# A message-passing network on one core: the messages' preparations move into the second convolution, and the edges' ends come in long rows that TensorE transposes

## The chip, the cores and the metric

The kernel runs on one core of a Trainium2 chip. The metric is the device time of one execution in microseconds (us). The engines are called PE (TensorE, the matrix engine; PEld is its weight load), DVE (VectorE), ACT (ScalarE), POOL (GpSimd) and SP (SyncE, which only issues transfers here). A PEq, ACTq or SPq in a row of the profile is that engine's issuing of a transfer.

## The reference

A graph of N = 6250 nodes with D = 64 features and E = 206250 directed edges (100,000 random pairs in both directions and a loop at each node), sorted by destination. Four layers, each behind a layer norm and a ReLU, each added to x:

```python
h = jnp.maximum(_layernorm(x, axis=-1), 0.0)
x = x + _L0_gnn_ref(h, edge_index, W3, b3, W4, b4)      # relu(S h W3' + b3) W4' through S again, S = D^-1/2 (A+I) D^-1/2
h = jnp.maximum(_layernorm(x, axis=-1), 0.0)
x = x + _L1_gnn_ref(h, edge_index)                      # sums over neighbours, scaled by deg^-1/2 on both sides
h = jnp.maximum(_layernorm(x, axis=-1), 0.0)
x = x + _L2_gnn_ref(h, edge_attr_64, src, dst, ...)     # messages, below
h = jnp.maximum(_layernorm(x, axis=-1), 0.0)
x = x + _L3_gnn_ref(edge_index, h)                      # three more neighbour sums (LightGCN), averaged
```

The third layer has work for each edge:

```python
Vp = leaky_relu(leaky_relu(V) @ pAw + pAb) @ pBw + pBb
x = relu(relu(E @ w1 + b1) @ w2 + b2)                   # E: 64 attributes of each edge
msg = sigmoid(x @ Bw + Bb) * Vp[src] + (x @ Cw + Cb)
M = clip(msg, 1e-5, None) ** 2
mean = segment_sum(M, dst) / max(cnt, 1)
return mean ** 0.5
```

## The kernel before

**Tiles.** Nodes are padded to 49 blocks (`NB`) of 128, in 7 chunks (`NC`) of 7 blocks (`CB`). A node matrix is a tile of 128 x 49 x 64. The graph is a dense matrix `A` of edge counts in fp8, in HBM, 7 column chunks of 128 x 49 x 896. A *piece* is one 7-block part of a chunk (784 KB). For the messages the edges are cut into 202 groups (`G`) of 1024: 128 partitions with 8 edges (`J`) each, consecutive in memory.

**Stages**, all in the function `fast`, with the times of the profiled execution:

1. *0 to 585 us.* `A` is built: pairs of source and destination go to HBM, runs of them are gathered, one-hot matrices are multiplied (L853), strips of `A` are evicted and stored (L984). On each strip the first convolution's neighbour sum runs (`convolve`, with `spread`, L748), then the hidden layer (`hidden`, L944 to L968); its last chunk ends the stage.
2. *585 to 806, gather 1* (the second convolution's neighbour sum). `gather` (L998) loops over 7 chunks of 7 pieces: SP loads a piece (L1007, eight buffers), PE multiplies it with node features split in three bf16 parts (L1013; L1010 is a multiplication with zeros that opens a bank), DVE sums the parts (L1021) and the function handed in, `convolved` (L1035), adds the bias and the residual and makes the next layer norm.
3. *806 to 1038, gather 2*, the same with `turned` (L1053): residual, layer norm (`normed`, L691 to L703), transposes (`p_node`, L1062), the two multiplications of Vp (`p_a` L1067, `p_v` L1073), the bias (`v`, L1076 and L1078) and the store of Vp to HBM (L1079).
4. *1038 to 1084, the preparations of the messages* (L1092 to L1157), below.
5. *1084 to 3670, the messages.* A schedule written by hand for PE, ACT and DVE: `slot(i)` for 202 groups in a pipeline seven deep. `loaded` brings edge attributes `e` (L1270, SP), `fetched` issues eight indirect transfers of Vp rows by `src_g` (L1276, POOL), `turned_edges` transposes `e` (`p_e`, L1284), two layers follow (L1288, L1292), gates and shifts (`p_bc`, L1298 and L1302), the message (DVE, L1311 to L1313), its sum by destination (`p_s`, L1330) with a one-hot matrix made of `lane` and `count`. Between these steps each slot takes a share of a list of other work: *crossings*, which compare pieces of `A` with their mirror images (`piece` L1177, `there` L1182, `p_sum` L1185, `junk` L1191), and partial sums of the first LightGCN layer. A chunk of nodes whose edges are all summed is `finished`.
6. *3670 to 4140.* The rest of LightGCN layer 1, and two more gathers.

`general`, which follows, runs only if `fast` has found that the graph isn't what it assumes; it isn't run here.

**The preparations.** ACT issues the loads of weights into diagonals (`w1_d`, `w2_d`) and `BC`, and eight small loads of biases (L1109, L1110); DVE splits the biases into three bf16 parts (L1113 to L1117); SP moves these to the rows of `BC_b` (L1120). SP loads the two index arrays, source and destination of each edge, group by group along a partition: partition p gets, of each of 202 groups, the 8 indices p·8 to p·8+7, so 128 x 202 runs of 32 bytes for each array:

```python
nc.sync.dma_start(src_g, src.rearrange("(g p j) -> p g j", p=P, j=J))
nc.sync.dma_start(dst_g, dst.rearrange("(g p j) -> p g j", p=P, j=J))
```

POOL writes `origin`, the first node of each group's window (194 memsets, L1133), and `count` (L1154). DVE makes from `dst_g` the check that all destinations lie in their windows (`rel`, `off`, `missed`, L1136 to L1142) and `lane` (L1145, L1147), all of 128 x 1616 elements.

**What sets the order.** Outside of the hand-written part the framework orders each engine's instructions by their dependencies and its own estimates; so preparations that wait for nothing are issued before gather 2's last chunk is through. An engine runs its instructions, the issuing of transfers among them, in that order and stops at the first that must wait. Tiles lie in pools. A pool opened where a closed one lay waits for all of that one's readers, writers and transfers. `cpool` (what the messages read) and `tpool` (what only the preparations need) lie where gather 2's buffers were.

Of the kernel before, what the change touches and what calls it, by code (L numbers as in the profile page):

```python
# [11 lines left out]
I32 = mybir.dt.int32  # L12
# [587 lines left out]
def window(g):  # L600

    per = N / E
    lo = max(int(g * P * J * per) - DRIFT, 0) // QN
    hi = min(int((g + 1) * P * J * per) + DRIFT, NP - 1) // QN
    assert hi - lo < P // QN
    return lo
# [10 lines left out]
def fast(ctx, tc, bad, x, src, dst, edge_attr, W3, b3, W4, b4, w1, b1, w2, b2, Bw, Bb, Cw, Cb,  # L617
# [48 lines left out]
    node = ctx.enter_context(tc.tile_pool(name="node", bufs=1))  # L666
    stat = ctx.enter_context(tc.tile_pool(name="stat", bufs=2))
# [84 lines left out]
    nc.scalar.dma_start(X, x.rearrange("(b p) f -> p b f", p=P))  # L752
    early = ExitStack()
    early_pool = early.enter_context(tc.tile_pool(name="early_pool", bufs=1))
    with ExitStack() as ph:

        ipool = ph.enter_context(tc.tile_pool(name="ipool", bufs=1))
        with ExitStack() as first:
            dpool = first.enter_context(tc.tile_pool(name="dpool", bufs=1))
# [37 lines left out]
        npool = looked.enter_context(tc.tile_pool(name="npool", bufs=1))  # L797
# [11 lines left out]
        rpool = ph.enter_context(tc.tile_pool(name="rpool", bufs=3))  # L809
        opool = ph.enter_context(tc.tile_pool(name="opool", bufs=2))  # L810
        spool = ph.enter_context(tc.tile_pool(name="spool", bufs=2))
        wpool = ph.enter_context(tc.tile_pool(name="wpool", bufs=1))
# [13 lines left out]
        with ExitStack() as ps:  # L826
            psum = ps.enter_context(tc.tile_pool(name="ps0", bufs=1, space=PSUM))
# [198 lines left out]

    with ExitStack() as ph:
        wpool = ph.enter_context(tc.tile_pool(name="wpool", bufs=2))  # L1030
        U3 = of_nodes(node)
        with tc.tile_pool(name="apool", bufs=8) as apool, \
                tc.tile_pool(name="ps1", bufs=1, space=PSUM) as psum:

            def convolved(c, z):  # L1035
                add_whole(z, V3, c)
                nc.vector.tensor_mul(z, z, over_features(norm0[:, blocks(c)]))
                nc.vector.tensor_add(z, z, over_blocks(b4_r, CB))
                nc.vector.tensor_add(X[:, blocks(c), :], X[:, blocks(c), :], z)
                h = wpool.tile([P, CB, D], F32, name="h")  # L1040
                normed_and_split(h, U3, c, norm3)

            gather(apool, wpool, psum, V3, convolved)
# [6 lines left out]
        with tc.tile_pool(name="apool", bufs=8) as apool, \  # L1050
                tc.tile_pool(name="ps2", bufs=1, space=PSUM) as psum:
# [34 lines left out]
    late = ctx.enter_context(tc.tile_pool(name="late", bufs=1))  # L1086
    H = late.tile([P, NB, D], F32, name="H")
    U3 = of_nodes(node)
    part = ctx.enter_context(tc.tile_pool(name="part", bufs=1))
    Y = part.tile([P, CS, CW], F32, name="Y")  # L1090
    piece_pool = ctx.enter_context(tc.tile_pool(name="piece_pool", bufs=3))
    with ExitStack() as ph:  # L1092
        cpool = ph.enter_context(tc.tile_pool(name="cpool", bufs=1))
        before = ExitStack()
        tpool = before.enter_context(tc.tile_pool(name="tpool", bufs=1))
        w1_d = diagonal(w1, "w1_d")
        w2_d = diagonal(w2, "w2_d")
        b1_c = column(b1, 2, "b1_c")
        b2_c = column(b2, 2, "b2_c")

        BC = cpool.tile([P, 4 * D], F32, name="BC")
        nc.vector.memset(BC, 0.0)
        for k in range(2):
            nc.scalar.dma_start(BC[k * D:(k + 1) * D, 2 * k * D:(2 * k + 1) * D], Bw)
            nc.scalar.dma_start(BC[k * D:(k + 1) * D, (2 * k + 1) * D:(2 * k + 2) * D], Cw)

        bias = tpool.tile([1, 4, 2, D], F32, name="bias")
        for k in range(4):
            nc.scalar.dma_start(bias[:, k, 0, :], Bb.unsqueeze(0))  # L1109
            nc.scalar.dma_start(bias[:, k, 1, :], Cb.unsqueeze(0))  # L1110
        rest = tpool.tile([1, 4, 2, D], F32, name="rest")
        bias3 = [tpool.tile([1, 4, 2, D], BF16, name=f"bias{k}") for k in range(3)]
        nc.vector.tensor_copy(bias3[0], bias)  # L1113
        nc.vector.tensor_sub(rest, bias, bias3[0])
        nc.vector.tensor_copy(bias3[1], rest)
        nc.vector.tensor_sub(rest, rest, bias3[1])
        nc.vector.tensor_copy(bias3[2], rest)  # L1117
        BC_b = cpool.tile([3, 8 * D], BF16, name="BC_b")
        for k in range(3):
            nc.sync.dma_start(BC_b[k:k + 1, :], bias3[k].rearrange("o a b f -> o (a b f)"))  # L1120
        ones = cpool.tile([3, P], BF16, name="ones")
        nc.vector.memset(ones, 1.0)

        src_g = cpool.tile([P, G, J], I32, name="src_g")
        nc.sync.dma_start(src_g, src.rearrange("(g p j) -> p g j", p=P, j=J))
        dst_g = tpool.tile([P, G, J], I32, name="dst_g")
        nc.sync.dma_start(dst_g, dst.rearrange("(g p j) -> p g j", p=P, j=J))

        origin = tpool.tile([P, G], F32, name="origin")
        g0 = 0  # L1130
        for g in range(1, G + 1):
            if g == G or window(g) != window(g0):
                nc.gpsimd.memset(origin[:, g0:g], float(window(g0) * QN))  # L1133
                g0 = g
        rel = tpool.tile([P, G, J], F32, name="rel")
        nc.vector.tensor_tensor(rel, dst_g, origin.unsqueeze(2).to_broadcast([P, G, J]),  # L1136
                                op=OP.subtract)
        off = tpool.tile([P, G, J], F32, name="off")
        nc.vector.tensor_scalar(off, rel, float(P), None, op0=OP.is_ge)
        nc.vector.tensor_scalar(rel, rel, 0.0, None, op0=OP.is_lt)  # L1140
        nc.vector.tensor_add(off, off, rel)
        nc.vector.tensor_reduce(missed[:, 1:2], off.rearrange("p g j -> p (g j)"), axis=AX.X,  # L1142
                                op=OP.add)

        nc.vector.tensor_scalar(dst_g, dst_g, P - 1, None, op0=OP.bitwise_and)  # L1145
        lane = cpool.tile([P, G, J], BF16, name="lane")
        nc.vector.tensor_copy(lane, dst_g)  # L1147
        own = cpool.tile([P, P // QN, 2], F32, name="own")
        nc.vector.memset(own[:, :, 0], 0.0)
        for q in range(P // QN):  # L1150
            nc.vector.memset(own[q * QN:(q + 1) * QN, :q + 1, 0], 1.0)
        nc.vector.tensor_scalar(own[:, :, 1], own[:, :, 0], -1.0, 1.0, op0=OP.mult, op1=OP.add)
        count = cpool.tile([P, P, J], BF16, name="count")
        nc.gpsimd.iota(count, pattern=[[1, P], [0, J]], base=0, channel_multiplier=0,  # L1154
                       allow_small_or_imprecise_dtypes=True)

        before.close()  # L1157
        mpool = ph.enter_context(tc.tile_pool(name="mpool", bufs=3))
        ps_a = ph.enter_context(tc.tile_pool(name="ps_a", bufs=1, space=PSUM))
# [255 lines left out]


# [87 lines left out]
```

## Time and profile before

| | us |
|---|---|
| median of 8 runs | 4152.68 |
| lowest, highest | 4138.55, 4200.15 |
| the profiled execution | 4141.91 |
| its span in the profile | 4140.0 |

Busy in the profiled span: PE 3170.8 us (77%), PEld 2173.4 (52%), DVE 1978.2 (48%), ACT 1258.3 (30%), POOL 1654.7 (40%). The granted TensorE clock is 0.85 of full speed on average.

The views used below are these. The *page's slices* cut the span in 40 equal parts, one digit each: the busy share in tenths (9 is 90% or more); PEclk is the TensorE clock that the throttle granted, DMA the mean busy share of the core's 16 DMA engines. *Busy time by stretch* gives for a stretch of the span each engine's busy us and its number of instructions, the granted clock, the DMA share and GB/s. The *timeline* has one row for a run of like instructions: start, length, engine, line, operation, output and inputs, count, and in brackets how long the engine stood idle before and what ended that. A busy time is not a bound: what a stage costs is read from the engine or transfer that the others wait for in that stage.

### The profile page before, as it was taken

How to read it: one execution, taken by the hardware profiler on the slowest of the kernel's cores; microseconds unless marked ns; L12 is line 12 of the kernel's file. 1: busy time of each engine (PE TensorE's matmuls, PEld its weight loads, DVE VectorE, ACT ScalarE, POOL GpSimd, SP SyncE). 2: the span in 40 equal slices, each digit the busy share in tenths (PEclk: the TensorE clock that was granted, in tenths of full speed). 3: DMA queues.
4: the chain of work that ended last, by engine and by line, in shares of the span. 5: the costliest groups of instructions: out<-in, count | busy, mean ns of one | idle time of the engine just before them, and what ended most of it. 6: DMA issues, size and time to landing. Idle time of an engine off the chain costs nothing.

```text
span 4140.0 us, 59188 instructions
## 1 busy us (share of the span) xinstructions
PE 3170.8 (77%) x24193; PEld 2173.4 (52%) x24193; DVE 1978.2 (48%) x3904; ACT 1258.3 (30%) x2031; POOL 1654.7 (40%) x1870
## 2 busy tenths in 40 slices
PE   1699999999366656777677677677767776789999
PEld 1466669999233333444333344344434343459999
DVE  5899953322344444545444444545445454461111
ACT  1577740000133333333333333333333333320000
POOL 4100000000466665665565666666566656510000
PEclk9799999999677777777877778878877788799999
DMA  3233346554722222222222222222222222236664
GB/s 102 71 83 88 100 147 196 183 183 132 93 58 58 60 58 55 74 66 72 56 58 78 57 66 68 65 73 61 75 58 64 60 74 63 53 107 194 196 202 151
DMA packets 280495, 388.75 MB, mean 94 GB/s; under 512 B 189225, under 2 KB 191331, under 8 KB 279955
## 3 DMA queue, kind: packets, MB, share of 16 engines
q1 hardware_dynamic: 222260, 323.17, 25.9%
q0 software_dynamic: 54112, 58.92, 7.2%
q8 instruction: 192, 3.15, 0.3%
q10 hardware_dynamic: 3840, 2.77, 0.3%
q14 instruction: 91, 0.75, 0.1%
HBM read 340.47 MB, written 44.24 MB: 93 GB/s over the span
## 4 chain that ended last, share of the span: by engine, by line
PE 51%; DVE 17%; another core or an unknown queue 12%; issue 9%; ACT 7%; DMA 2%; POOL 1%; DVEq 0%; ACTq 0%; POOLq 0%; SPq 0%
PE p_acc L1013 18%; PE p_sum L748 9%; PE p_bc L1302 6%; PE p L1288 5%; PE p_a L853 3%; ACT h L1292 2%; DVE junk L1191 2%; DVE m L1312 2%; DVE m L1311 2%; PE p_s L1330 2%; PE p_bc L1298 2%; PE p_e L1284 2%; DVE m L1313 1%; DVE m L1374 1%
## 5 line engine op out<-in xcount | busy, mean ns | idle before, releaser
L1276 POOL DMA_INDIRECT v<-Vp_dram,src_g x1616 | 1592.1, 985 | 997.9 <-DVE m L1311 490.0
L1013 PE MATMUL p_acc<-U,piece 128*128 128x192 bf16 x9604 | 816.8, 247 | 3.1 <-DMA piece<-A 3.1
L1013 PEld LDWEIGHTS <-piece 128*128 128x128 fp8e4 x9604 | 799.2, 98 | 14.8 <-DMA piece<-A 3.7
L1302 PE MATMUL p_bc<-BC,h 128*128 128x256 f32 x1616 | 580.2, 490 | 9.9 <-issue 9.6
L1311 DVE TENSOR_TENSOR m<-gate,v 128x512 f32<-128x512 f32 x202 | 139.9, 693 | 675.5 <-ACT gate L1307 472.0
L1302 PEld LDWEIGHTS p_bc<-BC,h 128*128 128x128 f32 x1616 | 339.5, 233 | 170.0 <-issue 132.7
L1185 PE MATMUL p_sum<-ident_b,piece 128*128 128x128 bf16 x1372 | 159.2, 240 | 337.8 <-DVE junk L1191 301.0
L1191 DVE SCALAR_TENSOR_TENSOR junk<-p_sum,there 128x512 bf16<-128x512 f32 (+1 forms) x392 | 241.9, 617 | 349.4 <-remote 249.8
L748 PEld LDWEIGHTS <-U 128*64 128x64 bf16 x4116 | 236.9, 114 | 316.1 <-issue 179.9
L1185 PEld LDWEIGHTS <-piece 128*128 128x128 fp8e4 x1372 | 120.0, 108 | 490.9 <-issue 474.6
L1133 POOL MEMSET origin<- 128x1 f32 (+1 forms) x194 | 6.5, 97 | 907.4 <-PE p_acc L1013 907.4
L1021 DVE TENSOR_REDUCE zg<-p_acc 128x128 f32<-128x384 f32 x112 | 56.9, 508 | 599.6 <-PE p_acc L1013 599.0
L857 ACT ACTIVATE strip<-p_a 128x784 fp8e4<-128x784 f32 x392 | 302.0, 820 | 120.8 <-PE p_a L853 103.7
L748 PE MATMUL p_sum<-piece,U 128*64 128x448 fp8e4 x2058 | 268.5, 387 | 89.7 <-issue 56.9
L1288 PE MATMUL p<-h,w_d 128*128 128x512 f32 x404 | 269.4, 750 | 63.0 <-ACT h L1292 53.6
L1292 ACT ACTIVATE h<-p,b_c 128x512 f32<-128x512 f32 x404 | 261.5, 683 | 173.1 <-remote 58.4
L1298 PE MATMUL p_bc<-BC_b,ones 3*128 3x512 bf16 x404 | 183.7, 455 | 135.9 <-DVE m L1312 129.0
L1330 PE MATMUL p_s<-m,to 128*128 128x192 bf16 x1616 | 207.9, 278 | 101.4 <-DVE r_s L1338 55.4
L1375 ACT ACTIVATE m<-m 128x512 bf16<-128x512 f32 x202 | 127.3, 630 | 520.5 <-DVE m L1374 390.6
L1318 ACT ACTIVATE m<-m 128x512 bf16<-128x512 f32 x202 | 127.2, 630 | 434.2 <-DVE m L1313 341.3
L1298 PEld LDWEIGHTS <-ones 3*128 3x128 bf16 x404 | 37.6, 93 | 417.6 <-issue 216.5
L1288 PE MATMUL p<-eT,w_d 128*128 128x512 f32 x404 | 246.6, 695 | 11.9 <-ACT h L1292 7.1
(189 smaller groups left out, 3650.8 us busy)
## 6 DMA issues: line engine op xcount, KB each, us to landing
piece<-A SPq DMA_DIRECT2D x249, 784.0 KB
e<-in_edge_attr SPq DMA_DIRECT2D x202, 256.0 KB
A<-strip SPq DMA_DIRECT2D x14, 2744.0 KB
v<-Vp_dram,src_g POOLq DMA_INDIRECT x1616
there<-A SPq DMA_DIRECT2D x28, 784.0 KB
pairs<-pair SPq DMA_DIRECT2D x1, 1616.0 KB
Vp_dram<-v SPq DMA_DIRECT2D x7, 224.0 KB
out<-X SPq DMA_DIRECT2D x6, 224.0 KB
```

What stands on the lines that cost most here:

```text
L748: nc.tensor.matmul(p[half * D:(half + 1) * D, :w], U3[:, b, k, :], at_block, start=(i < 2), stop=(i >= 3 * n - 2))
L857: nc.scalar.activation(strips[s][:, :, col:col + 2 * SG].rearrange("p b (j l) -> p b j l", l=2), p[:, :, :2 * NB].rearrange("p j (b l) -> ...
L1013: nc.tensor.matmul(p[d // 2][:, d % 2 * 3 * D:(d % 2 + 1) * 3 * D], t[:, b, d * P:(d + 1) * P], U3[:, k * CB + b, :, :].rearrange("p t f - ...
L1185: nc.tensor.matmul(p[:, a - a0, :], held["here"][:, a, b * P:(b + 1) * P], ident_b, start=True, stop=True)
L1191: nc.vector.scalar_tensor_tensor(junk[:, :(a1 - a0) * P], p[:, :a1 - a0, :].rearrange("p a q -> p (a q)"), 15.5, there, op0=OP.min, op1=OP ...
L1276: nc.gpsimd.indirect_dma_start(out=v[:, j, :], out_offset=None, in_=Vp_dram[:, :], in_offset=bass.IndirectOffsetOnAxis(ap=src_g[:, g, j:j ...
L1288: nc.tensor.matmul(of[g][p], w, of[g].pop(x), start=True, stop=True)
L1292: nc.scalar.activation(of[g][t], of[g].pop(p), **how)
L1298: nc.tensor.matmul(p_bc[:, 4 * b:4 * b + 4].rearrange("p j o f -> p (j o f)"), ones, BC_b, start=True, stop=False)
L1302: nc.tensor.matmul(p_bc[:, 2 * q:2 * q + 2].rearrange("p j o f -> p (j o f)"), h2[:, q * P:(q + 1) * P], BC, start=False, stop=(k == 1))
L1311: nc.vector.tensor_mul(m, of[g].pop("gate"), of[g].pop("v"))
L1330: nc.tensor.matmul(p, to[:, :, j], m3[:, j].rearrange("p t f -> p (t f)"), start=(j == 0), stop=(j == J - 1))
```

## The change

The preparations become a function, `prepared(psum)`, which `convolved` calls when it gets chunk 1 of gather 1. Its tiles lie at the other end of SBUF (`side="right"`), and `cpool` stays open until the messages are over. The transfers into `BC_b` are issued by ACT instead of SP. The index arrays come as rows: a group is one row of 1024 indices, 4 KB; 101 groups, half an array, are one transfer, issued by ACT. DVE casts such a half to float32 with the 8 indices of a partition drawn apart, PE transposes it in eight pieces of 101 x 128, four to a PSUM bank (32 transposes in all), and ACT writes each four back as integers into `src_g` or `dst_g`. All that follows from these two tiles is as it was. Beside that, all pools of `fast` get `reuse_waits="tile"`: a tile waits for those earlier tiles whose memory it takes, no longer for the whole closed pool; and `spool` (the strips of `A`) goes to the right side.

```diff
-    node = ctx.enter_context(tc.tile_pool(name="node", bufs=1))
-    stat = ctx.enter_context(tc.tile_pool(name="stat", bufs=2))
+    node = ctx.enter_context(tc.tile_pool(name="node", bufs=1, reuse_waits="tile"))
+    stat = ctx.enter_context(tc.tile_pool(name="stat", bufs=2, reuse_waits="tile"))
...
+    apart = ctx.enter_context(ExitStack())
     early = ExitStack()
...
-        spool = ph.enter_context(tc.tile_pool(name="spool", bufs=2))
+        spool = ph.enter_context(tc.tile_pool(name="spool", bufs=2, side="right", reuse_waits="tile"))
...
+    def prepared(psum):
+
+        cpool = apart.enter_context(tc.tile_pool(name="cpool", bufs=1, side="right", reuse_waits="tile"))
+        before = ExitStack()
+        tpool = before.enter_context(tc.tile_pool(name="tpool", bufs=1, side="right", reuse_waits="tile"))
+        w1_d = diagonal(w1, "w1_d")
...
+        BC_b = cpool.tile([3, 8 * D], BF16, name="BC_b")
+        for k in range(3):
+            nc.scalar.dma_start(BC_b[k:k + 1, :], bias3[k].rearrange("o a b f -> o (a b f)"))
...
+        src_g = cpool.tile([P, G, J], I32, name="src_g")
+        dst_g = tpool.tile([P, G, J], I32, name="dst_g")
+        GH = G // 2
+        for ends, t in ((src, src_g), (dst, dst_g)):
+            for h in range(2):
+                rows_i = tpool.tile([GH, P, J], I32, name="rows_i", bufs=2)
+                nc.scalar.dma_start(rows_i, ends[h * GH * P * J:(h + 1) * GH * P * J].rearrange(
+                    "(g p j) -> g p j", p=P, j=J))
+                rows_f = tpool.tile([GH, J, P], F32, name="rows_f", bufs=2)
+                nc.vector.tensor_copy(rows_f, rows_i.rearrange("g p j -> g j p"))
+                for j0 in range(0, J, 4):
+                    p = psum.tile([P, 4, GH], F32, name="p_turn", bufs=2)
+                    for j in range(4):
+                        nc.tensor.transpose(p[:, j, :], rows_f[:, j0 + j, :], ident[:GH, :GH])
+                    nc.scalar.activation(
+                        t[:, h * GH:(h + 1) * GH, j0:j0 + 4],
+                        p.rearrange("p j g -> p g j"), AF.Copy)
...
+        before.close()
+        return cpool, w1_d, w2_d, b1_c, b2_c, BC, BC_b, ones, src_g, lane, own, count
+
+    made = []
...
             def convolved(c, z):
+                if c == 1:
+                    made.append(prepared(psum))
                 add_whole(z, V3, c)
...
-        BC_b = cpool.tile([3, 8 * D], BF16, name="BC_b")
-        for k in range(3):
-            nc.sync.dma_start(BC_b[k:k + 1, :], bias3[k].rearrange("o a b f -> o (a b f)"))
...
-        src_g = cpool.tile([P, G, J], I32, name="src_g")
-        nc.sync.dma_start(src_g, src.rearrange("(g p j) -> p g j", p=P, j=J))
-        dst_g = tpool.tile([P, G, J], I32, name="dst_g")
-        nc.sync.dma_start(dst_g, dst.rearrange("(g p j) -> p g j", p=P, j=J))
...
+        cpool, w1_d, w2_d, b1_c, b2_c, BC, BC_b, ones, src_g, lane, own, count = made.pop()
+        mpool = ph.enter_context(tc.tile_pool(name="mpool", bufs=3, reuse_waits="tile"))
...
+    apart.close()
```

## The prediction

> **What bounds the kernel now.** I read the page's slices first, to see which engine fills which stage, then busy time by stage, then the timeline at the two seams that the change touches.
>
> ```profile
> PE   1699999999366656777677677677767776789999
> DVE  5899953322344444545444444545445454461111
> PEclk9799999999677777777877778878877788799999
> DMA  3233346554722222222222222222222222236664
> ```
>
> A slice is 103.5 us. Counted from 1, TensorE (PE) is full in slices 3 to 10 (first convolution, then the two gathers) and in the last four (layers); slices 12 to 36, the messages, have no full engine. Slice 11 is the hole: PE 3, and DMA 7, the highest of its row. The stages in numbers (after span and length: PE, PE weight loads, DVE, ACT, POOL busy; granted clock; DMA share; GB/s):
>
> ```profile
> 580.00:815.00 235.00, 225.96 (x2560) 217.04 (x2554) 78.75 (x145) 14.17 (x28) 0.00 (x0) 0.96 0.56 184
> 1040.00:1120.00 80.00, 22.44 (x79) 12.48 (x79) 19.91 (x40) 6.46 (x11) 36.28 (x180) 0.60 0.90 110
> 1120.00:1320.00 200.00, 125.48 (x501) 70.89 (x502) 86.48 (x189) 66.75 (x112) 124.83 (x129) 0.72 0.23 58
> 1320.00:3600.00 2280.00, 1616.63 (x7468) 900.02 (x7468) 1097.99 (x2422) 773.50 (x1293) 1412.67 (x1431) 0.79 0.25 64
> ```
>
> Gather 1 is PE's own: 226 of 235 us. What the change puts on PE there lengthens it; what it puts on DVE (79 of 235 busy) or POOL (0) does not. The stretch before the messages is bound by DMA. Its timeline (start, us, engine, line, operation, idle before):
>
> ```profile
> 1038.26 0.39 SPq L1125 DMA_DIRECT2D src_g<-in_src  x1
> ...
> 1042.80 10.30 SPq L1127 DMA_DIRECT2D dst_g<-in_dst  x1
> ...
> 1055.93 0.23 ACTq L1109 DMA_DIRECT2D bias<-in_L_gnn_Bb  x1
> 1056.20 0.27 ACTq L1110 DMA_DIRECT2D bias<-in_L_gnn_Cb  x1
> 1056.51 0.30 ACT L701 ACTIVATE v<-v,eps 128x7 f32<-128x7 f32 x1 [42.09 <-DMA bias<-in_L_gnn_Bb]
> ...
> 1070.48 1.84 DVE L1136 TENSOR_TENSOR rel<-dst_g,origin 128x1616 f32<-128x1616 int32 x1 [4.89 <-DMA dst_g<-in_dst]
> 1072.24 0.55 DVE L1076 TENSOR_TENSOR v<-p_v,pBb_r 128x384 f32<-128x384 f32 x1
> ...
> 1072.94 0.39 SPq L1079 DMA_DIRECT2D Vp_dram<-v  x1
> ...
> 1081.01 0.98 POOL L1276 DMA_INDIRECT v<-Vp_dram,src_g  x1 [34.27 <-DMA piece<-A]
> ...
> 1083.92 1.09 PE L1284 MATMUL p_e<-ident,e 128*128 128x128 f32 x4 [16.14 <-DMA e<-in_edge_attr]
> ```
>
> The two 32-byte-run loads fill the DMA engines from 1038 to 1070. ACT stands behind its small bias transfers until 1056.5, and the square root (L701) of gather 2's last chunk stands behind them; then `v` (L1076) stands on DVE behind `rel`, which waits for dst_g. So the last store of Vp goes out at 1072.94, and every fetch of a message needs it.
>
> **The change, part by part.** Sums are against the profiled execution's own 4141.91 us (span 4140.0 and 1.91 around it).
>
> *(a) Start of the messages, a gain.* All that delays the chain is gone from its place. Without it the chain of the chunk before is the model: reduce at 1004.80, Vp store at 1017.12, 11.4 us from its last reduce's end (1005.73). The last chunk's reduces end at 1038.6; PE is cold there (p_node 1.09 against 0.66, p_a 2.07 against 1.12, p_v 2.04 against 1.16), so 2.3 more: store at 1052.3 instead of 1072.94. The first fetch came 8.07 us after that store, part of it behind DVE's preparations (to 1080.2) and e's loads on SP (1080.25); without them the store's landing is left, 2.4 us after its issue (SP's first piece, at 1075.34, waited for it), so some 3 us with the fetch's own start. First fetch ≈ 1055.5 instead of 1081.0: **−25.3**. Bounds: −32, if PE stays warm and e, which no longer waits for DVE, puts the first slots ahead of the fetch; −8, if a stall further on takes the place of the hole (rival 1). I take −25.3, as every row of the chain exists one chunk earlier. In the built order every engine but SP runs the messages in the same sequence, so I expect their 2586 us (1084 to 3670) to shift, not change.
>
> *(b) First convolution to gather 1, a loss.* Now:
>
> ```profile
> 585.33 23.61 SPq L1007 DMA_DIRECT2D piece<-A  x9
> ...
> 600.72 0.62 DVE L966 TENSOR_TENSOR z<-p_node,norm 128x448 f32<-128x448 f32 x1 [11.79 <-PE p_node L962]
> ...
> 601.82 2.40 PE L1013 MATMUL p_acc<-U,piece 128*128 128x192 bf16 x14
> ```
>
> The preparations are called at c = 1, but what waits for nothing is placed earlier: in the built order five of the 32 transposes stand on PE between the zeros and gather 1's first matmul. They wait for DVE's first cast of long rows, and DVE has eight operations ahead of it after z (601.34): four of split (0.62 each, two of them behind ACT's 0.58) and four of the bias (0.42, 0.68, 0.41, 0.68): 4.7, with gaps some 5.3, then the cast, 0.65 (0.99 for 128x1616 of L776, by length). PE begins transposing at ≈ 607, five at the cold 0.27 (1.09/4): first matmul ≈ 608.4, **+6.6**. Bounds: +3 (the casts fall into split's gaps), +10 (the cast at twice the price, its long rows landing late). Of the piece loads, eight of the first eleven now wait on ACT's small or long-row transfers; PE needs a new piece every 4.1 us (29 us a chunk of seven), and the first four land by ≈ 603 by their waits: hidden. ACT issues 19 transfers at 0.23 to 0.63 in its gaps of 1.7 to 2.2 us: hidden as well.
>
> *(c) End of chunk 1, a loss.* The other 27 transposes stand among the first matmuls of chunk 2, at 0.165 each (four in 0.66, warm): 4.5 us. Sets of four wait for ACT's eviction two sets back (0.60 each) and two sets wait for a cast: ≈ 2 more. **+6.5**, bounds +4.5 and +10. DVE's ≈ 12 us (1.84, 1.84, 1.83, four of 0.99, two casts) lie in a chunk of 29 us in which it is a third busy; POOL's 6.51 and 1.94 have an idle engine. Without that cover, gather 1's last reduces would come 12 us late.
>
> The Trainium skill, "TensorE: Matmul & The Clock Gate", part 4, gives about 275 ns for a transpose inside a kernel (bf16, 128x128) and says that transposes don't count as PE work for its clock. By that figure the 32 would cost 8.8 us instead of 5.9; the four-in-0.66 rows here are of float32 and cheaper, and I stay with them.
>
> *(d) Pools that wait tile by tile.* At the very start pair's operations go ahead of a normalisation on DVE, and `near` no longer waits for the landing of pairs' tail (25.73 to 27.27): **−2.9**, bounds 0 and −5. Between the gathers nothing moves: gather 2's first piece takes the buffer of gather 1's last (49 mod 8 = 1). At the messages' end PE stands idle 10 us (3670.8 to 3680.75) for the last `finished`; that chain remains: **−0.5**, bounds 0 and −1.
>
> Sum: −25.3 + 6.6 + 6.5 − 2.9 − 0.5 = **−15.6**, 4126.3 for an execution like the profiled one. That one lies 10.8 below the median of the eight runs (4152.68; 4138.55 to 4200.15), so the median I forecast is **4137**. All bounds together give −30.5 (−32 + 3 + 4.5 − 5 − 1) to +12 (−8 + 10 + 10): 4122 to 4165.
>
> **The rivals.**
> 1. *The early start is not kept* (0.17). From 1106 to 1124 of before, DVE waits 18.2 us for a crossing, ACT 12.7 for `eT` and PE 6.2 for nothing shown, with DMA at a share of 0.1: a stall without a named cause. If its end is fixed by something that doesn't move with Vp (instructions being loaded, say), up to 17 of (a) go into it: −16 + 14 = −2, **4151**. Against: it sits among the first slots, whose work is the same and moves as a whole.
> 2. *Slower: SP in order behind ACT* (0.08). Gather 1's pieces go out in order, and each of eight stands behind a transfer that ACT issues only when its own waits are over. At 4.1 us a piece PE has little in hand; the sum without this is −15.6, so it turns at 2 us a stop. At 4.5 us a stop: +36 − 15.6 = +20, **4173**. Against: stops overlap with eight buffers, and they end with the eleventh of 49 pieces.
> 3. *A slower slot* (0.10). Tiles of the messages lie elsewhere in SBUF and start in another phase to their transfers; 0.08 us a slot (of 12.8) in 202 eats the gain, 0.2 gives +25, **4178**; over 1% from 0.28. Nothing in the order speaks for it.
> 4. *The stall goes, or the clock is back sooner* (0.10). The same 18 us could vanish with the transfers before it: −34, **4119**; or the first 200 us run at 0.79 instead of 0.72, and 125 us of PE shrink by 11: 4126. No row gives a reason for either. On the clock the same skill page, part 1, lets a pause of some 3.4 us halve it; two such pauses remain, so by it nothing is gained.
>
> **How the numbers follow.** Forecast 0.55, rivals 0.17, 0.08, 0.10, 0.10. About 1% (41 us) is what a measurement of this kernel can tell from no change. Forecast, rival 1 and most of 4 lie within; over 1% slower needs the upper halves of 2 and 3, faster both parts of 4 (−45) or chance between medians whose runs lie 62 us apart. Faster 0.07, same 0.85, slower 0.08. Range: 4110, where most of rival 4 is in, to 4168, with all of rival 1 and a part of 2 and 3.
>
> **What would show it.** Right: last Vp store at ≈ 1062 on the new time axis (1052 plus the ≈ 10 of b to d), first fetch 3 us later, no DMA-bound hole before the messages; gather 1's first matmul ≈ 6 us after z, its length ≈ 248 instead of 235 with 32 transposes in it; slots of 12.8 as before. Wrong: a hole that stays though src_g is early, PE waiting for pieces in chunk 1 or 2, or a message stage whose length moves by more than 5 us.

## The result and the profile after

The changed kernel takes 4177.48 us (median; 4153.69 to 4205.27) where the kernel before takes 4155.19 (median over all its runs). The ratio is 1.0055, with a 95% interval from 1.0035 to 1.0074: slower by about 23 us. The same comparison on another occasion gave 1.0051 (1.0020 to 1.0083). That lies within the 1% that the prediction called "same", but outside its range and on the other side: 4137 was forecast. The profiled execution's span is 4175.3 us.

The rows of the page's slices (40 equal parts of the span, each 104.4 us here):

```profile
PE   1699977999666666777677666766776677789999
DVE  5899953322144454445544444544454454462111
PEclk9699988999777777887777787877777887899999
DMA  3233334555322222222222222222222222235664
```

The hole of before is gone: slice 11 has PE 6 and DMA 3 where it had 3 and 7. But in slices 6 and 7, the start of gather 1, PE fell from 9 to 7, and the granted clock to 8. Busy time by stretch (columns as before: start and length, PE, PE weight loads, DVE, ACT, POOL, clock, DMA share, GB/s):

```profile
580.00:815.00 235.00, 189.60 (x2056) 179.05 (x2053) 74.82 (x132) 15.81 (x31) 1.94 (x1) 0.87 0.49 168
...
1120.00:1320.00 200.00, 119.53 (x494) 66.58 (x494) 82.20 (x180) 65.58 (x108) 130.76 (x135) 0.74 0.23 60
1320.00:3600.00 2280.00, 1586.22 (x7341) 882.80 (x7340) 1079.60 (x2389) 761.91 (x1277) 1401.42 (x1422) 0.78 0.25 64
```

PE does 189.6 us of work in a stretch where it did 226: 36 us lost in the stage that PE bounds. The timeline says to what:

```profile
597.59 0.26 ACTq L1067 DMA_DIRECT2D rows_i<-in_src  x1
...
601.60 2.76 ACTq L1067 DMA_DIRECT2D rows_i<-in_src  x1
...
618.46 1.08 DVE L1070 CAST rows_f<-rows_i 101x1024 f32<-101x1024 int32 x1 [12.23 <-DMA rows_i<-in_src]
...
619.60 1.10 PE L1074 MATMUL p_turn<-ident,rows_f 101*128 101x101 f32 x5 [16.55 <-DVE rows_f L1070]
620.50 17.95 PE L1014 MATMUL p_acc<-U,piece 128*128 128x192 bf16 x196
...
639.48 1.08 DVE L1070 CAST rows_f<-rows_i 101x1024 f32<-101x1024 int32 x1 [19.62 <-DMA rows_i<-in_src]
...
648.27 13.68 PE L1014 MATMUL p_acc<-U,piece 128*128 128x192 bf16 x147 [9.81 <-DMA piece<-A]
671.06 2.42 PE L1014 MATMUL p_acc<-U,piece 128*128 128x192 bf16 x14 [8.95 <-DMA piece<-A]
...
689.83 0.50 PE L1014 MATMUL p_acc<-U,piece 128*128 128x192 bf16 x2 [4.07 <-DMA piece<-A]
```

The first load of long rows is issued at 597.59 and has landed when its cast starts, at 618.46: 20.9 us for 404 KB, where a piece of 784 KB takes 4.3 (the one issued at 608.63 in the kernel before has landed at 612.97). The second lands 21 us after the first. PE stands before its five early transposes for 16.6 us and then, three times, for pieces, 22.8 us together. Chunks 0 and 1 end 47.1 us late: 18.7 of it is the late first matmul (620.5 instead of 601.8), 22.8 are the waits for pieces, and the other 5.6 go to slower matmuls, at a granted clock of 0.83 from there to the end of chunk 1 instead of 0.96.

Why are the pieces late? SP loads them in order, and a piece load that is given the semaphore of an earlier transfer (the counter that tells of a landing) stands until that transfer has landed. What SP waited for from 585 to 700 (us in total, times, longest), three lines of that view:

```profile
SPq L1008 <- DMA rows_i<-in_dst: 43.3, 2, 21.8
...
SPq L1008 <- DMA BC_b<-bias: 20.4, 1, 20.4
SPq L1008 <- DMA rows_i<-in_src: 19.8, 1, 19.8
```

`BC_b` is a small transfer that ACT issued behind the second load of long rows, and it lands 0.2 us after that load, at 639.65. These are the issue times of the first eighteen piece loads, read one by one from the three traces (the third kernel is the first experiment below):

```
before                585.3 585.7 586.2 586.7 587.3 587.8 588.4 588.9 608.6 612.7 616.7 620.8 624.8 628.8 632.9 637.6 641.6 645.7
changed               593.9 598.3 618.5 618.9 639.7 640.1 640.6 662.5 662.9 663.4 685.6 686.0 686.5 687.0 687.7 688.2 688.7 689.2
changed, 96 + 5 rows  593.0 597.3 602.0 608.2 608.6 609.1 609.5 610.9 613.2 617.3 621.3 625.3 629.4 633.4 637.5 642.2 646.2 650.3
```

In the changed kernel SP issues in four bursts some 21 us apart (618.5, 639.7, 662.5, 685.6): the beat of the four long-row transfers, not of PE, which uses up a piece in 4.1 us.

At the start of the messages the change does what was expected of it:

```profile
1088.14 0.94 DVE L1022 TENSOR_REDUCE zg<-p_acc 128x128 f32<-128x384 f32 x2 [0.60 <-PE p_acc L1014]
...
1093.26 0.30 ACT L701 ACTIVATE v<-v,eps 128x7 f32<-128x7 f32 x1 [28.38 <-DVE v L700]
...
1102.90 0.37 SPq L1166 DMA_DIRECT2D Vp_dram<-v  x1
...
1106.19 0.98 POOL L1299 DMA_INDIRECT v<-Vp_dram,src_g  x1 [518.39 <-issue]
...
1149.87 0.69 DVE L1334 TENSOR_TENSOR m<-gate,v 128x512 f32<-128x512 f32 x1 [22.48 <-ACT gate L1330]
```

ACT's square root now waits for DVE, not for a transfer. The ledger of the two profiled executions, from start times in the traces:

| us | before | changed | difference |
|---|---|---|---|
| end of gather 1's chunk 0 / 1 / 2 | 632.9 / 661.8 / 690.8 | 662.0 / 708.9 / 741.4 | +29.1 / +47.1 / +50.6 |
| end of gather 2 (last reduce) | 1038.3 | 1088.7 | +50.4 |
| from there to the last Vp store | 34.6 | 14.2 | −20.4 |
| from there to the first fetch | 42.7 | 17.5 | −25.2 |
| from there to the first message product | 90.2 | 61.2 | −29.0 |
| first to last sum of messages (`p_s`) | 2525.2 | 2541.1 | +15.9 |
| last sum to the end | 474.0 | 472.2 | −1.8 |

Up to the first message product the change costs 50.4 − 29.0 = +21.4, close to the difference of the medians (22.3). The 15.9 of the messages can't be told from scatter: nine profiles at this speed, of kernels that differ in what stands ahead of the messages, gave 2525 to 2579 us, and the same kernel profiled twice gave 2541 and 2556 (the changed one) and 2579 and 2549 (that of experiment 1). The prediction's sign of being wrong, a message stage that moves by more than 5 us, is finer than two single profiles can show.

### The profile page after: what moved, and what is told of

Same layout as the page of the kernel before. It is cut to its first block, busy times and chain, and to the rows that moved or that the text cites. A ratio compares the mean times of both kernels' runs of the same rounds, so it can differ in the third digit from the quotient of the medians.

```text
span 4175.3 us, 59226 instructions
## 1 busy us (share of the span) xinstructions
PE 3167.3 (76%) x24225; PEld 2172.8 (52%) x24225; DVE 1979.4 (47%) x3908; ACT 1261.0 (30%) x2039; POOL 1653.3 (40%) x1870
## 4 chain that ended last, share of the span: by engine, by line
PE 49%; DVE 17%; another core or an unknown queue 13%; issue 9%; ACT 7%; DMA 3%; POOL 1%; ACTq 1%; DVEq 0%; POOLq 0%; SPq 0%
PE p_acc L1014 17%; PE p_sum L748 10%; PE p_bc L1325 6%; PE p L1311 5%; PE p_a L854 3%; DVE junk L1214 3%; ACT h L1315 2%; DVE m L1334 2%; DVE m L1335 2%; PE p_s L1353 2%; PE p_bc L1321 2%; PE p_e L1307 1%; DVE m L1336 1%; DVE m L1397 1%
## 5 line engine op out<-in xcount | busy, mean ns | idle before, releaser
L1325 PE MATMUL p_bc<-BC,h 128*128 128x256 f32 x1616 | 559.0, 476 | 12.4 <-issue 12.2
L1325 PEld LDWEIGHTS p_bc<-BC,h 128*128 128x128 f32 x1616 | 327.6, 225 | 164.3 <-issue 130.0
L748 PE MATMUL p_sum<-piece,U 128*64 128x448 fp8e4 x2058 | 291.8, 399 | 124.7 <-issue 76.0
L748 PE MATMUL p_sum<-strip,U 128*64 128x448 fp8e4 x2058 | 241.1, 362 | 10.4 <-ACT U L711 4.6
```

The source lines that it names most:

```text
L748: nc.tensor.matmul(p[half * D:(half + 1) * D, :w], U3[:, b, k, :], at_block, start=(i < 2), stop=(i >= 3 * n - 2))
L1325: nc.tensor.matmul(p_bc[:, 2 * q:2 * q + 2].rearrange("p j o f -> p (j o f)"), h2[:, q * P:(q + 1) * P], BC, start=False, stop=(k == 1))
```

## The experiments

Three chips took part. On two the kernel before takes 4150 to 4190 us, on the third 3640; the messages take 2065 us there instead of some 2540 (in the three kernels profiled on it). So ratios are only taken within a chip, and otherwise times of the stages before the messages are compared, which agree across the chips to a few us.

**Theory:** the 101 rows of a half are carried by one of the 16 DMA engines, and PE, DVE and SP stand in order behind their landing. **Rivals:** SP stands behind ACT's late issuing, whatever the transfers' speed; or the tile-by-tile pools or the tiles' places cost the time.

**1. Each half in 96 rows and 5**

```diff
-                nc.scalar.dma_start(rows_i, ends[h * GH * P * J:(h + 1) * GH * P * J].rearrange(
-                    "(g p j) -> g p j", p=P, j=J))
+                for r0, r1 in ((0, 96), (96, GH)):
+                    nc.scalar.dma_start(
+                        rows_i[r0:r1], ends[(h * GH + r0) * P * J:(h * GH + r1) * P * J].rearrange(
+                            "(g p j) -> g p j", p=P, j=J))
```

> The changed kernel with each half's 101 long rows loaded by two transfers, of 96 rows and of 5. Theory (a transfer of 101 rows is carried by one DMA engine, since 101 divides into no smaller parts: 404 KB in 17 to 21 us): the rows land in 2 to 4 us, the first five transposes come at about 607 instead of 619.6, PE waits for pieces less than 3 us in chunks 0 and 1 instead of 23, gather 2's last reduce is at about 1051 instead of 1088.7, and the time is 38 us below the changed kernel's, near 4140, ratio to before about 0.996. Rival (SP's piece loads wait in order behind transfers that ACT issues late; their speed doesn't matter): PE still waits 15 us and more for pieces, the time stays within 8 us of the changed kernel's.

Measured: ratio to before 0.9954 (0.9920 to 0.9989), and in a second comparison 0.9948 (0.9922 to 0.9975): 20 us faster than before, some 42 below the changed kernel. Its timeline:

```profile
604.68 1.06 DVE L1072 CAST rows_f<-rows_i 101x1024 f32<-101x1024 int32 x1
...
605.80 1.10 PE L1076 MATMUL p_turn<-ident,rows_f 101*128 101x101 f32 x5 [3.67 <-DVE rows_f L1072]
...
606.70 18.54 PE L1014 MATMUL p_acc<-U,piece 128*128 128x192 bf16 x195
```

The cast has nothing to wait for, the transposes come at 605.8, and in the whole of gather 1 there is no stop of PE over 1.5 us but the seam to gather 2. Chunk 0 ends at 637.5 (+4.6 to before), chunk 2 takes 3.5 more than the others, gather 2 ends at 1046.3 (+8.0), the first product is at 1108.8 (−19.7). SP stands in order behind ACT's transfers in this kernel as well, but from 595 on for 5.8 us at most. So the first rival falls: the extra issues and waits are hidden if the transfers are quick.

**2. Only the pools**

All pools of `fast` get the tile-by-tile reuse, and `spool` goes to the right side, in the kernel before:

```diff
-        opool = ph.enter_context(tc.tile_pool(name="opool", bufs=2))
-        spool = ph.enter_context(tc.tile_pool(name="spool", bufs=2))
+        opool = ph.enter_context(tc.tile_pool(name="opool", bufs=2, reuse_waits="tile"))
+        spool = ph.enter_context(tc.tile_pool(name="spool", bufs=2, side="right", reuse_waits="tile"))
...
```

> The kernel before with the tile-by-tile pools and the strips on the right side, nothing else. Theory (the pools do nothing that counts; the message stage's longer 16 us in the changed kernel's profile is run-to-run): z of the last hidden chunk at 600.5 to 601, gather 2's last reduce within 3 us of 1038.3, time within 0.2% of before. Rival (the new waits or places of tiles slow the messages): the stage from the first message product to the last is 2540 instead of 2524 us and the time 14 us up; prediction's own term: 2.9 us faster at the start.

Measured: ratio 0.9985 (0.9958 to 1.0011), no difference that shows. Gather 2 ends at 1038.4 (before 1038.3); from there to the first product it takes 84.1 us instead of 90.2. The messages of the profiled execution, the slowest of ten, took 2579 us, more than the rival asks; but the ten together are not slower. This rival falls too: no loss comes from the pools. The term of 2.9 us for the start isn't there either. `near` is loaded 2.1 us earlier (25.21 instead of 27.27), but the layer norm (z, L696) now waits for the landing of pairs, whose tile it overlaps, and its operations then stand on DVE ahead of what uses `near`: `begin` comes at 42.07, before at 41.92.

**3. Moved, but in the old short runs**

```diff
-        GH = G // 2
-        for ends, t in ((src, src_g), (dst, dst_g)):
...
+        nc.scalar.dma_start(src_g, src.rearrange("(g p j) -> p g j", p=P, j=J))
+        nc.scalar.dma_start(dst_g, dst.rearrange("(g p j) -> p g j", p=P, j=J))
```

> The changed kernel's preparations at their new place, but the index arrays loaded in the old 32-byte runs, by two transfers from ACT, without rows, casts, transposes and evictions. Theory (what is heavy in the old loads is their packets, 30 us of all 16 DMA engines): DMA is at 0.9 for some 30 us at the start of gather 1, its pieces wait, chunk 0 ends 20 to 35 us later than the 632.9 of before, and the time is within 12 us of before, 25 above the 96-and-5 kernel. Rival (DMA is idle enough there to hide them): chunk 0 ends within 8 us of before and the time is 20 to 25 us below before.

Measured: 4168.66 in a single execution, beside a median of 4184.0 for before, no more than those runs scatter. The stages: chunk 0 ends at 657.8 (+24.9), PE stops for 7.2 and 13.9 us at 617.0 and 643.1, gather 2 ends at 1064.0 (+25.7). The busy time by stretch shows the DMA engines full, from 590 to 660 (a packet counts whole in the stretch in which it starts, so a share can pass 1):

```profile
590.00:630.00 40.00, 28.60 (x216) 23.68 (x217) 6.87 (x20) 3.50 (x6) 0.00 (x0) 0.70 0.99 164
630.00:660.00 30.00, 16.10 (x177) 15.41 (x175) 12.59 (x14) 0.00 (x0) 0.00 (x0) 0.78 1.25 214
```

The first product is at 1126.5, 2 us earlier than before: the short runs cost in gather 1 what they had cost ahead of the messages. To move them is to move the hole. SP's pieces stand in order behind these landings too (18.5 us for `src_g`, 24.8 for `dst_g`), so the run doesn't tell how much is the full engines and how much the order.

**4. The transfers by themselves**

A kernel of its own, whose core is:

```
def long_rows(r, engine=nc.scalar):
    engine.dma_start(R[:r], src[:r * P * J].rearrange("(g p j) -> g p j", p=P, j=J))
...
for i in range(3):
    for r in (128, 112, 101, 100, 96, 64):
        long_rows(r)
        nc.vector.tensor_copy(seen[:r], R[:r, 0, 0:1])
        nc.vector.tensor_copy(R[:, 0, 0:1], seen)
```

After these it loads 128 rows of 6 KB three times, meant to be alone, and then three times each beside 101 and beside 96 long rows.

> Nothing of the network is computed: the kernel copies part of x to the output and loads rows of 4 KB, one transfer after the other, of 128, 112, 101, 100, 96 and 64 rows, then a load of 128 rows of 6 KB alone, beside a load of 101 rows, and beside one of 96. Theory (one DMA engine for 101): 101 rows take 15 to 20 us from issue to landing, 100 rows some 3, 96, 64, 112 and 128 rows 2 to 3; the 6 KB load takes 4 us alone, under 6 beside 96 rows, and 10 to 20 beside 101, because the one engine that carries the rows owes it its share too. Rival (4 KB rows are slow as such, or only the wait's order counts): 101 is within 10% per row of 96 and 100, and the 6 KB load lands in 4 to 6 us beside either.

In the timeline, DVE's idle time before each row runs from about the issue of a load to its landing. Below it are two stretches (length; DVE, ACT and POOL busy; clock; DMA share; GB/s), the first inside a load of 101 rows, the second inside one of 100:

```profile
39.69 0.15 DVE L64 CAST seen<-R 101x1 f32<-101x1 int32 x1 [18.33 <-DMA R<-in_src]
...
44.11 0.15 DVE L64 CAST seen<-R 100x1 f32<-100x1 int32 x1 [4.08 <-DMA R<-in_src]
...
47.80 0.15 DVE L64 CAST seen<-R 96x1 f32<-96x1 int32 x1 [3.35 <-DMA R<-in_src]
```

```profile
24.00:38.00 14.00, 0.00 (x0) 0.00 (x0) 0.00 (x0) 1.00 0.06 26
41.00:43.50 2.50, 0.00 (x0) 0.00 (x0) 0.00 (x0) 1.00 0.51 161
```

A load of 101 rows is waited for 18.1 to 18.3 us (three times), 100 rows 3.8 to 4.1, 96 rows 3.3 to 3.4, 64 rows 3.5 to 3.8, 112 and 128 rows 3.4 to 3.5 (these two from the second round on; the first ran beside the copy of x). The DMA share during the 101 rows is 0.06, that is 1/16, at 26 GB/s. One row more than 100 makes the transfer 4.6 times as long. The Trainium skill states the rule: in "DMA: Bandwidth & Descriptors", section "Why a DMA increments its semaphore by 16 and not by 1", a transfer gets the largest number of engines up to 16 that divides the sizes of the slowest dimension on both sides; its examples are 100 partitions, 10 engines, and 127, one. 101 is a prime: one engine. The share here agrees.

The last part of the theory holds in kind, not in size. No large load ran alone: the first stood beside the copy of x, and the first 101 rows of this part were issued at 128.02, ahead of the loads meant to be alone, and landed at 153.8. So five large loads ran beside 101 rows and were waited for 7.1 to 8.5 us, three ran beside 96 rows, 6.0 to 6.2:

```profile
136.04 0.16 DVE L52 TENSOR_TENSOR seen<-seen,B 128x1 f32<-128x1 f32 x1 [7.87 <-DMA B<-in_edge_attr]
...
201.38 0.16 DVE L52 TENSOR_TENSOR seen<-seen,B 128x1 f32<-128x1 f32 x1 [5.99 <-DMA B<-in_edge_attr]
```

The first of these loads in two stretches shows what the 101 rows cost it:

```profile
128.30:132.30 4.00, 0.00 (x0) 0.00 (x0) 0.00 (x0) 1.00 0.60 199
132.30:135.90 3.60, 0.00 (x0) 0.00 (x0) 0.00 (x0) 1.00 0.06 26
```

Most of it moves in four microseconds; for the other 3.6 only one engine's worth is busy, with packets of both transfers. In the changed kernel the same is seen at the pieces. The trace records 16 completions of a piece, one for each engine. Of the piece issued at 639.71, 15 have come by 644.56, the last comes at 648.22, and PE goes on at 648.27; of that issued at 685.61, beside no long rows, the last comes 0.1 us after the fifteenth. So the changed kernel's pieces are late mainly because they are issued late; but the last 3.7 us of PE's first two stops for pieces (9.8 and 9.0 us) are the wait for the one engine that carries the rows.

**5. The long rows without the move**

In the kernel before, only the two loads are replaced, by rows of 96 and 5 issued by SP, with casts, transposes (in a PSUM pool of their own) and evictions:

```diff
-        nc.sync.dma_start(src_g, src.rearrange("(g p j) -> p g j", p=P, j=J))
...
+                    for r0, r1 in ((0, 96), (96, GH)):
+                        nc.sync.dma_start(
+                            rows_i[r0:r1], ends[(h * GH + r0) * P * J:(h * GH + r1) * P * J].rearrange(
+                                "(g p j) -> g p j", p=P, j=J))
...
```

> The kernel before, its pools and the place of its preparations unchanged; only the loads of the index arrays are the long rows (96 and 5 from SP), with casts, transposes and evictions. Theory (the hole before the messages was made by the 30 us of short packets, not by the preparations' place): last Vp store at 1053 to 1060 instead of 1072.9, first fetch at 1060 to 1068 instead of 1081, first message product at 1108 to 1116 instead of 1128.5, time 13 to 20 us below before; so the move itself adds 5 us or less. Rival (the place counts: transposes, casts and DVE's 12 us stand in the chain there): first product at 1123 or later.

Measured on the third chip: ratio 0.9979 (0.9969 to 0.9988), 7.6 us faster. From gather 2's last reduce it is 15.9 us to the Vp store (34.6 before, 14.2 changed), but 32.9 to the first fetch:

```profile
1047.77 0.40 SPq L1079 DMA_DIRECT2D Vp_dram<-v  x1
1047.89 6.23 PE L1140 MATMUL p_turn<-ident,rows_f 101*128 101x101 f32 x32 [0.87 <-DVE v L1078]
...
1064.83 0.98 POOL L1292 DMA_INDIRECT v<-Vp_dram,src_g  x1 [23.63 <-DVE missed L1158]
```

The transposes, evictions and DVE's checks stand between the store and the fetch, since the old pools let no message tile begin before `missed`. The two edits are worth little one at a time: the rows 7.6 us, the move (with its pools) nothing that shows (experiment 3). My theory that the move adds 5 us or less is wrong; beside the seam kernel of experiment 6, on the same chip, it adds some 13 by the ratios.

**6. Transposes at the seam**

The 96-and-5 kernel, with the loads tied to chunk 5's sums and the transposes called in chunk 6 (`prepared` as a generator, rows_i in 3 buffers, rows_f in 4):

```diff
+                nc.vector.tensor_copy(rows_i[:, 0, 0:1], z[:GH, 0, 0:1])
                 for r0, r1 in ((0, 96), (96, GH)):
...
+                turns.append((t, h, rows_f))
+        yield
+        for t, h, rows_f in turns:
             for j0 in range(0, J, 4):
...
-                if c == 1:
-                    made.append(prepared(psum))
+                if c == NC - 2:
+                    steps.append(prepared(psum, z))
+                    next(steps[0])
+                if c == NC - 1:
+                    next(steps[0], None)
```

> The 96-and-5 kernel with the row loads tied to chunk 5 of gather 1 (a one-column write into each row tile, from that chunk's sums, before its load) and the 32 transposes called in chunk 6, so that they stand between the gathers, where PE waits 4.6 us for a piece anyway. Theory (what is left of the loss is the five transposes that stand ahead of gather 1, 4.9 us, and 3.6 in chunk 2): gather 1 starts at 602 and ends at 806 to 808, the seam grows by 1 to 3 us, gather 2's last reduce is at 1039 to 1042 (1046.3 with 96 and 5, 1038.3 before), first product at about 1103, time 24 to 28 us below before, ratio 0.994. Rival (PE stops for casts and evictions in the seam as long as it saved): last reduce at 1046 or later, ratio as with 96 and 5.

> The changed kernel beside the next two on one chip. Theory: 20 to 25 us above before.

> The changed kernel with 96 and 5 rows, beside the others on one chip. Theory: 14 to 20 us below before, some 40 below the changed kernel.

> The kernel with transposes at the seam, beside the others on one chip. Theory: 4 to 7 us below 96 and 5, 20 to 26 below before.

Measured: 0.9944 (0.9930 to 0.9957) on the third chip. On one of the other two, beside the rest: changed 1.0051 (1.0020 to 1.0083), 96 and 5 0.9948 (0.9922 to 0.9975), seam 0.9908 (0.9882 to 0.9934). It is the fastest of all, 20 us below before on the one chip and 38 on the other; the size isn't settled better than that, its stages ahead of the messages (gather 2 ends at 1035.3, the 96-and-5 kernel's at 1043.7) account for 8 of the 16 us between the two. The expectation was 4 to 7 us below 96 and 5, and the last reduce at 1039 to 1042. Its seam:

```profile
804.60 0.86 PE L1081 MATMUL p_turn<-ident,rows_f 101*128 101x101 f32 x8
...
808.04 0.97 PE L1081 MATMUL p_turn<-ident,rows_f 101*128 101x101 f32 x8 [0.19 <-ACT dst_g L1082]
...
809.13 1.33 PE L1014 MATMUL p_acc<-U,piece 128*128 128x192 bf16 x14
```

Between the last matmul of gather 1 and the first of gather 2 are 4.6 us, as before; the 32 transposes fit into the wait for the piece and cost nothing.

**7. Slow rows that nobody needs yet**

Two kernels load the undivided 101 rows in chunk 0, with the transposes at the seam, to separate SP's waiting from PE's. In the first the casts followed the loads; in the second they are tied to chunk 6 too, and rows_i has four buffers. The edit of the first, in the seam kernel, and what the second adds to it:

```diff
-                for r0, r1 in ((0, 96), (96, GH)):
+                for r0, r1 in ((0, GH),):
...
-                if c == NC - 2:
+                if c == 0:
```

```diff
-                rows_f = tpool.tile([GH, J, P], F32, name="rows_f", bufs=4)
-                nc.vector.tensor_copy(rows_f, rows_i.rearrange("g p j -> g j p"))
-                turns.append((t, h, rows_f))
+                turns.append((t, h, rows_i))
...
+            rows_f = tpool.tile([GH, J, P], F32, name="rows_f", bufs=2)
+            nc.vector.tensor_copy(rows_f[:, 0, 0:1], z[:GH, 0, 0:1])
+            nc.vector.tensor_copy(rows_f, rows_i.rearrange("g p j -> g j p"))
```

> The seam kernel with undivided loads of 101 rows, tied to chunk 0 of gather 1; nothing needs the rows until 806, some 170 us later. Theory (a slow transfer costs because SP's piece loads, which reuse its semaphore, wait for its landing in order, whoever needs the rows): the four rows land at about 651, 669, 687 and 706, pieces 19 to 22 are issued only then, PE stands idle 10 to 18 us in chunk 3, and gather 1 ends 10 to 18 us later than 806. Rival (in the changed kernel only PE's own wait for the rows counted, the piece waits followed from it): no idle time over 2 us in chunks 1 to 5, gather 1 ends within 3 us of 806.

> As the kernel with undivided early loads, but the casts too are tied to chunk 6 (a one-column write from that chunk's sums), so that no engine needs the rows before the seam: the only one that waits for a landing is SP, where a piece load reuses the semaphore of a row load. Theory: the rows land some 19 us apart, at about 50, 69, 89 and 109 us after gather 1's first matmul; pieces 18, 19, 21 and 22 are issued only then; PE stands idle 15 to 25 us in chunk 3 with DMA piece as what it waited for, and the gather ends that much later. Rival (DVE's or PE's own wait for the rows is needed for a loss): no idle time over 2 us in chunks 1 to 5.

Measured, one execution each: the first stops PE for 64.0 us at 654.5, far more than expected. DVE's four casts stand in its queue ahead of the rest of `convolved`, each waits for a landing (651.6, 670.3, 691.3, 709.9), and the reduces that free PE's banks come after them. The second stops PE once in chunks 1 to 5, for 23.6 us at 659.2; the size is in the expected 15 to 25, the cause only in part:

```profile
635.68 41.71 ACTq L1070 DMA_DIRECT2D rows_i<-in_dst  x2
...
677.44 0.30 ACT L701 ACTIVATE v<-v,eps 128x7 f32<-128x7 f32 x1 [76.78 <-issue]
...
682.81 0.48 PE L1011 MATMUL p_acc<-zeros,ident_b 128*128 128x384 bf16 x1 [23.63 <-DVE zg L1022]
682.81 0.10 PEld L1014 LDWEIGHTS <-piece 128*128 128x128 fp8e4 x1 [23.78 <-DMA piece<-A]
```

SP's pieces are held as the theory has it (issued at 655.9, 674.6, 695.5 and 714.0, about 20 us apart). But ACT is held as well: to issue its third and fourth row loads takes it 25.4 and 16.2 us (the 41.71 of the first line). The trace names no semaphore that ends these, so why an issue behind long rows lasts so long stays open. ACT's square root stands behind that, DVE behind the square root, and PE behind DVE. So the two causes fall together, and how much SP alone would cost isn't separated. Nobody needs the rows for 170 us, and the slow transfers still cost 24: what pays is every queue that has something in order behind them.

## Why the prediction was wrong

| term | forecast | measured in the changed kernel | with 96 and 5 rows |
|---|---|---|---|
| (a) to the first fetch / first product | −25.3 | −25.2 / −29.0 | −25.5 / −27.7 |
| (b) gather 1's start and chunks 0 and 1 | +6.6 | +47.1 | +4.6 |
| (c) chunk 2 | +6.5 | +3.5 | +3.5 |
| (d) pools, start | −2.9 | +0.3 | +0.1 |
| (d) end | −0.5 | −1.8 | −1.4 |

The measured (d) at the start is contained in the measured (b).

*(a)* was right, by its own steps: the store 13.8 us after the end of the last reduce (forecast 13.7), the fetch 3.3 later (forecast 3). Its subtraction slips by 0.2 (1055.5 less 1081.0 is −25.5), which changes nothing. The stall at 1106 to 1124 of before (rival 1) took nothing back.

*(b)* is the step that failed, in what it put at nothing: "the first four land by ≈ 603 by their waits: hidden". It gives the landing of a long-row load no price of its own, and its upper bound of +10 leaves a few microseconds for "its long rows landing late"; both hold only if 404 KB in 101 rows land about as fast as a piece. Each such load takes about 21 us, carried by one engine of 16, so the third piece was issued at 618.5, and (b) cost 47.1 us instead of 6.6. No row of the trace of before shows such a transfer: every large load in it goes over 128 rows. The rest of the step was right: with quick rows the five transposes come at 605.8 (forecast 607) and the first matmul at 606.7 (forecast 608.4). The cast was underpriced (1.08 us instead of 0.65).

*Rival 2* named the place (SP in order behind transfers that ACT issues, in the first eleven pieces). That its 4173 lies near the measured 4177 is luck: it counted eight stops of 4.5 us, and there were four of SP, of 20 to 22 us each, of which PE felt a part. It got 0.08, since a stop's price was taken from transfers that were quick. It also left out that PE's early transposes and DVE's casts wait for the same landing, ahead of the pieces.

*(c)* was too dear: its 27 transposes lengthen chunk 2 by 3.5 us. In experiment 6 eight of 101 x 101 take 0.86 to 0.97 us, 0.11 to 0.12 each, not the 0.165 of a 128 x 128. The about 275 ns that the Trainium skill gives in "TensorE: Matmul & The Clock Gate", part 4, for a 128 x 128 transpose in bf16 is more than either of these float32 rows shows. *(d)* missed a wait that the reuse of memory by tile adds (the layer norm behind the landing of pairs). Of rivals 3 and 4 no run shows anything beyond the scatter of the messages; a slot that is slower by a few hundredths of a microsecond isn't excluded, but it isn't needed for the loss.

## What to carry to other kernels

Before a transfer is priced by its bytes, look at the number of rows it goes over: 101 rows of 4 KB took 18 us, 100 took 4, 96 under 3.5. A slow transfer is paid not only where its data is used, but by each engine whose queue has something that waits for it, its semaphore included, and by each transfer that needs the DMA engine it holds; so ask of a moved load who stands in order behind its landing. And two edits to one hole may be worth little each (7.6 us and nothing that shows) and 20 together: a hole goes when the last thing in it goes.

## What was not expected of the hardware

One transfer of 101 rows leaves the other 15 DMA engines free (share 0.06), and still delays a load that needs all 16: 15 parts of a piece land, and the sixteenth comes 3.4 to 6.5 us later while the rows are on their way. The same program ran in 3640 us on one chip and 4150 to 4190 on two others: the stages before the messages agree to a few us, the messages take 2065 against some 2540 us, with a mean granted clock of 0.90 against 0.85 over the span. PE's largest group of the messages costs about the same per instruction (498 ns in the seam kernel on the one chip, 484 on another), and PE's busy time in the stage differs by some 115 us (1670 and 1785), so most of the difference is waiting; why was not found.
